# Forming the weight sums in feed-forward block 0 instead of block 1, so that nine blocks of layer 0 use seven products instead of eight

## Chip, cores and metric

The kernel runs on one core of one Trainium2 chip. The metric is the device time of one execution in microseconds (us). Three runs of the kernel before took 1858.07, 1859.28 and 1859.49 us; the median is 1859.28. The execution that was profiled is the one of 1859.49.

## What is computed

Two layers of a graph transformer on N = 2708 tokens with 512 features, 8 heads of 64 and a hidden width of 2048, in float32. Each token attends only to the tokens that the adjacency matrix joins it with (a handful each). Cut to one layer:

```python
q = (h @ Wq.T + bq); k = (h @ Wk.T + bk); v = (h @ Wv.T + bv)      # 8 heads of 64
scores = q k^T / sqrt(64), and -1e9 where adj + eye is 0
ctx = softmax(scores) v
h1 = layer_norm(h + ctx @ Wo.T + bo)
h2 = layer_norm(h1 + relu(h1 @ W1.T + b1) @ W2.T + b2)
```

Layer 1 does the same to the result of layer 0, with its own weights.

## The kernel before

**Tiles and stages.** The tokens are sorted by their number of neighbours and cut into 22 tiles of 128 (the last has 20). In the first stage (up to about 250 us) the kernel finds each token's neighbours and projects keys, values and queries of layer 0. Then comes layer 0's feed-forward, in eleven blocks of two tiles each, numbered k = 0 to 10; the last has the tile of 20 tokens. The loop over blocks is at the end of `by_edges`; inside it, `f` runs over the 16 slices of 128 hidden features. Layer 1 follows in the same manner.

**Attention is interleaved by hand.** The order of instructions on every engine is the order in which the Python code issues them; nothing reorders it. `attend` is a generator. One step of it takes up to two gathered neighbours of each token of a tile (`SLOTS = 2`): VectorE multiplies keys by the query (L1150) and sums within heads (L1156), and weights the values of the step before (L1182, L1189); ScalarE takes the exponentials (L1169) and weights half of the values (L1176). A step is about 4.3 us of VectorE's queue, or 2.7 if it has one neighbour. After a tile's last step come its sums (L1197 to L1212) and, one step later, the division on ScalarE (L1220), which makes the tile's context `cx`. `advance(...)` issues steps after slice f by a credit: the table `PACES` gives it in block 0, `PACE` in other blocks of plain products, and `PACE7` in blocks of seven products; at most three contexts may be ahead. `until(g)` issues whatever steps are missing for tile g.

**A block, on TensorE.** For each slice f, four matmuls make `pf` (L1516 in a plain block, L1648 in a block of seven products) and ScalarE evicts it with a ReLU into `ft` (L1527, L1659). PSUM has three places for `pf` in plain blocks and two in the others. Beside this, each block carries work for its neighbours: at f = 5 to 8 the block before it is finished (its result z is turned, `tp` L1285; then keys and values of layer 1, `k` and `v` at L620, added to their bias by VectorE at L1728 and copied by ScalarE at L1733); from f = 10 the contexts of the next block's two tiles are turned (`tp<-cx`, copied by ScalarE to `cT`, L1290), multiplied by Wo (`o`, L620), added to the residual (`h`, L1447) and normalised (L1269 to L1279); and at f = 15 `h` is turned for the next block. z and h are both called `h` in the profile.

**The second product.** The product with W2 sums over the 16 slices. In a plain block (`feed_forward`), each slice and tile is one matmul of 512 columns (L1489). A block of seven products (`feed_forward_by_seven`) takes slices in pairs j = 0 to 6, and does the 2 x 2 block product of a pair (two tiles by two halves of the columns) with seven matmuls of 256 columns (L1638) instead of the eight that four of 512 columns amount to. The last pair is done plainly (L1670, L1674). For this it needs

- sums of the weights, made once: `form(j)`, four VectorE instructions on 128 x 256 (L1587 to L1590), one of which overwrites a part of W2's tile, and three stores on the SP queue to `form_d` (L1592); each block of seven products loads them back (`ask_forms`, L1605), three of 128 KB for each pair, through three places in SBUF;
- sums of the hidden values, in every such block: `sums(j)`, four VectorE additions of 128 x 128 for each pair (L1620 to L1623), issued at the next even f;
- a tail of eight VectorE instructions (L1693 to L1700), where a plain block has two (L1562).

**Where it is set.** `FORMED` is the block in which the weight sums are formed, after slices f in `FORMS` = (3, 5, 7, 9, 11, 13, 15); blocks FORMED + 1 to 9 then use seven products. It stands in the loop over blocks in four ways:

```python
seven = n == 0 and FORMED < k < NB - 1
if n == 0 and k == FORMED:
    now.prepared()
if n == 0 and k in (FORMED + 1, NB - 1):
    places_of_psum(3 - seven, seven)
...
if n == 0 and k == FORMED and f in FORMS:
    now.form(FORMS.index(f))
```

The first three lines of the loop's choice follow from `seven`: which product is used, which pace (`PACE7 if seven else ...`), and how many PSUM places there are.

Of the kernel before, what the change touches and what calls it, by code (L numbers as in the profile page):

```python
# [52 lines left out]
    (0.75,) * 11 + (0.0,) * 2 + (0.9,) * 3,  # L53
)
PACE7 = (0.0,) * 4 + (0.6, 1.0, 1.5, 1.5, 0.8, 0.7, 0.8, 0.0, 0.0, 0.6, 0.8, 1.4)
FORMED = 1
FORMS = (3, 5, 7, 9, 11, 13, 15)
PACE = (
    (0.0,) * 2 + (0.6,) * 3 + (1.2,) * 4 + (0.6,) * 2 + (0.0,) * 2 + (0.8,) * 3,
# [424 lines left out]
def by_edges(ctx: ExitStack, tc: tile.TileContext, x, xT, adj, layers, out, redo):  # L484
# [34 lines left out]
    def places_of_psum(n, more=False):  # L519

        nonlocal ps_f, ps, ps_s
        stage.close()
        ps_f = stage.enter_context(tc.tile_pool(name="ps_f", bufs=n, space=PSUM))
        ps = stage.enter_context(tc.tile_pool(name="ps", bufs=n, space=PSUM))
        if more:
            ps_s = stage.enter_context(tc.tile_pool(name="ps_s", bufs=1, space=PSUM))
# [767 lines left out]
    class Layer:  # L1294
# [313 lines left out]
        def feed_forward_by_seven(self, k, block, hs, hT):  # L1608
# [5 lines left out]
            fts = []  # L1614
            base = 3 * J * (k - FORMED - 1)

# [259 lines left out]
    for n in range(NL):  # L1876
# [47 lines left out]
        for k, block in enumerate(blocks):  # L1924
# [3 lines left out]
            if n > 0 and 0 < k < NB - AHEAD:  # L1928
                asking = now.queries(blocks[k + AHEAD])
# [5 lines that stand above are left out]
# [4 lines left out]
            for f, zs in enumerate(working):  # L1939
# [25 lines left out]
                if n > 0 and (k, f) == (0, 2):  # L1965
                    now.load_second(1, temp)
                if n == 0 and k == FORMED and f in FORMS:
                    now.form(FORMS.index(f))
# [109 lines left out]
```

## Time and profile before

| | before |
|---|---|
| median of 3 runs | 1859.28 us |
| profiled execution | 1859.49 us |
| its span | 1857.8 us |
| TensorE (PE) busy, share of the span | 1817.6 us, 98% |
| VectorE (DVE) busy | 1460.0 us, 79% |
| ScalarE (ACT) busy | 951.7 us, 51% |
| GpSimd (POOL) busy | 800.3 us, 43% |
| mean granted TensorE clock | 0.991 |
| layer 0's blocks 0 to 9, first matmul of block 0 to first of block 10 | 249.97 to 1034.82 us |

The span is the profiled execution's time on the engines; 1.7 us of the measured time lie around it. The profile cuts the span into 40 slices of 46.4 us and gives each engine's busy share of a slice in tenths (9 is 90% or more). A line of a timeline gives start, duration, engine, line of the code, operation, output and inputs, shapes, the number of records merged in it, and in brackets the idle time before it with what ended that. Each float32 matmul of the program shows as two records. `PEld` are weight loads, `SP` the queue from which most plain transfers are issued.

### The profile page before, as it was taken

Reading aid. Unit: us, or ns where it says so; the run is one execution under the profiler, and the core shown is the slowest. Engines: PE = TensorE matmul, PEld = TensorE weight load, DVE = VectorE, ACT = ScalarE, POOL = GpSimd, SP = SyncE. Lnnn points to the kernel's source line nnn. Section 1 sums busy time; section 2 is a strip of 40 time slices with the busy share of each in tenths; the row PEclk is TensorE's granted clock in tenths of the full one; section 3 lists DMA queues with packets and bytes.
Section 4 is the critical chain, followed back from the end, with each engine's and each line's share of the span. In section 5 each row is a group of like instructions: output and inputs, shape, how many; then the busy total and the mean of one; then the engine's idle time right before and its main releaser. Section 6 shows DMA issues by size and latency. Waiting matters only on the chain.

```text
span 1857.8 us, 22528 instructions
## 1 busy us (share of the span) xinstructions
PE 1817.6 (98%) x6563; PEld 1167.4 (63%) x6563; DVE 1460.0 (79%) x2447; ACT 951.7 (51%) x3271; POOL 800.3 (43%) x745
## 2 busy tenths in 40 slices
PE   9999999999999999989997999999999999999998
PEld 4444466567776777758675644666666666666666
DVE  4986878888978888888878237877988898989853
ACT  4770445545545465454454214555655675566531
POOL 3334755535445454454432013535454554455302
PEclk9999999999999999999998999999999999999999
DMA  9987986756666565665654578735645573655400
GB/s 338 377 329 262 369 273 236 255 173 228 203 201 233 188 215 182 216 211 186 207 157 133 191 245 315 288 132 189 224 162 195 198 261 133 223 194 175 138 23 21
DMA packets 158062, 393.82 MB, mean 212 GB/s; under 512 B 17514, under 2 KB 60894, under 8 KB 157928
## 3 DMA queue, kind: packets, MB, share of 16 engines
q0 software_dynamic: 70608, 252.12, 39.4%
q1 hardware_dynamic: 77162, 118.55, 18.5%
q10 hardware_dynamic: 10158, 21.61, 3.1%
q8 instruction: 54, 0.88, 0.2%
q14 instruction: 80, 0.66, 0.1%
HBM read 338.78 MB, written 53.44 MB: 211 GB/s over the span
## 4 chain that ended last, share of the span: by engine, by line
PE 82%; DVE 9%; ACT 4%; issue 2%; DMA 1%; POOL 1%; POOLq 0%; DVEq 0%; ACTq 0%
PE pf L1516 17%; PE a L1489 16%; PE pf L1648 8%; PE q L620 8%; PE o L620 7%; PE k L620 7%; PE v L620 7%; PE c L1638 4%; PE a L1638 3%; PE tp L1285 2%; DVE sc L1156 2%; DVE kv L1150 2%; ACT kv L1176 1%; DVE acc L1189 1%; ACT cx L1220 1%
## 5 line engine op out<-in xcount | busy, mean ns | idle before, releaser
L1113 POOL DMA_INDIRECT kv<-kv_d,listed x420 | 523.4, 1246 | 331.9 <-DVE acc L1189 161.1
L1516 PE MATMUL pf<-hT,w 128*128 128x256 f32 (+1 forms) x1792 | 393.3, 367 | 0.1
L1516 PEld LDWEIGHTS pf<-hT,w 128*128 128x128 f32 x1792 | 323.5, 190 | 103.2 <-issue 64.4
L1489 PE MATMUL a<-w,ft 128*128 128x512 f32 x800 | 373.2, 592 | 0.0
L1176 ACT ACTIVATE kv<-kv,p 128x64 f32<-128x64 f32 x1232 | 311.0, 335 | 5.0
L1275 POOL TENSOR_TENSOR rd<-va,mhalf 128x1 f32<-128x1 f32 (+1 forms) x88 | 79.6, 905 | 521.2 <-DVE va L1273 521.1
L1150 DVE TENSOR_TENSOR kv<-kv,q 128x1024 f32<-128x1024 f32 (+1 forms) x222 | 256.8, 1157 | 15.0 <-DMA q<-q_d,ident_i 11.1
L1156 DVE TENSOR_REDUCE sc<-kv 128x16 f32<-128x1024 f32 (+1 forms) x222 | 257.9, 1162 | 7.6
L1189 DVE TENSOR_TENSOR acc<-acc,kv 128x1024 f32<-128x1024 f32 (+2 forms) x178 | 205.3, 1153 | 43.6 <-ACT kv L1176 28.3
L1648 PE MATMUL pf<-hT,w 128*128 128x256 f32 x1024 | 232.9, 379 | 0.0
L1489 PEld LDWEIGHTS a<-w,ft 128*128 128x128 f32 x800 | 150.2, 190 | 113.2 <-issue 101.3
L1648 PEld LDWEIGHTS pf<-hT,w 128*128 128x128 f32 x1024 | 194.0, 190 | 33.3 <-issue 8.1
L1527 ACT ACTIVATE ft<-pf,b 128x256 f32<-128x256 f32 (+1 forms) x208 | 94.7, 458 | 196.1 <-PE pf L1516 196.0
L1169 ACT ACTIVATE p<-sc,listed 128x8 f32<-128x8 f32 x420 | 104.4, 297 | 162.1 <-DVE sc L1156 132.9
L620 PE MATMUL o<-wo,cT 128*128 128x512 f32 x336 | 152.8, 599 | 6.5 <-ACT cT L1290 6.5
L1182 DVE TENSOR_TENSOR kv<-kv,p 128x512 f32<-128x512 f32 (+1 forms) x178 | 123.4, 693 | 17.7 <-ACT p L1169 17.7
L1659 ACT ACTIVATE ft<-pf,b 128x256 f32<-128x256 f32 x96 | 44.8, 467 | 152.2 <-PE pf L1648 152.2
L620 PEld LDWEIGHTS o<-wo,cT 128*128 128x128 f32 x336 | 64.0, 192 | 81.9 <-issue 65.7
L1279 DVE SCALAR_TENSOR_TENSOR h<-h,rd,ln_b 128x512 f32<-128x512 f32 (+1 forms) x88 | 66.1, 751 | 46.2 <-POOL rd L1275 46.2
L745 DVE MAX8 tops<-code 128x8 f32<-128x247 f32 (+2 forms) x242 | 79.0, 400 | 28.0 <-ACT code L740 26.0
L1220 ACT ACTIVATE cx<-acc,su 128x64 f32<-128x64 f32 (+1 forms) x352 | 88.2, 333 | 13.9 <-DVE su L1212 10.7
L1447 DVE TENSOR_TENSOR h<-o,xb 128x512 f32<-128x512 f32 (+1 forms) x44 | 30.2, 687 | 76.1 <-PE o L620 67.2
(231 smaller groups left out, 2340.7 us busy)
## 6 DMA issues: line engine op xcount, KB each, us to landing
aj<-in_adj SPq DMA_DIRECT2D x42, 677.0 KB, 6.4
forms<-form_d SPq DMA_DIRECT2D x168, 128.0 KB, 4.0
kv_d<-kvs ACTq DMA_DIRECT2D x21, 512.0 KB, 6.6
xg<-in_xT SPq DMA_DIRECT2D x19, 512.0 KB, 7.3
w<-in_W SPq DMA_DIRECT2D x16, 512.0 KB, 6.2
kv<-kv_d,listed POOLq DMA_INDIRECT x420, 6.1
zT_d<-zT SPq DMA_DIRECT2D x22, 256.0 KB, 6.1
xb_d<-h SPq DMA_DIRECT2D x21, 256.0 KB, 6.0
```

The source lines that it names most:

```text
L620: nc.tensor.matmul(o[:r], xs(c), wm[:, c, :], start=(c == 0), stop=(c == NC - 1))
L1113: return nc.gpsimd.indirect_dma_start(out=to, out_offset=None, in_=table[:, :], in_offset=bass.IndirectOffsetOnAxis(ap=s, axis=0), bounds_ ...
L1150: nc.vector.tensor_tensor(kv[:r, :c, :DM], kv[:r, :c, :DM], self.q[:r].unsqueeze(1).to_broadcast([r, c, DM]), ALU.mult,)
L1156: nc.vector.tensor_reduce(self.sc[:r, s0 : s0 + c, :], kv[:r, :c, :DM].rearrange("p s (h d) -> p s h d", d=DK), AX.X, ALU.add,)
L1176: nc.scalar.activation(to[:, i, hd], kv[:r, i, DM + h * DK : DM + (h + 1) * DK], AF.Copy, scale=p[:r, s0 + i, h : h + 1],)
L1182: nc.vector.tensor_tensor(to[:, 0, :].rearrange("p (h d) -> p h d", d=DK), kv[:r, 0, DM:].rearrange("p (h d) -> p h d", d=DK), p[:r, s0, : ...
L1189: nc.vector.tensor_tensor(self.acc[:r, :c, :], self.acc[:r, :c, :], kv[:r, :c, DM:], ALU.add)
L1220: nc.scalar.activation(cx[:r, hd], self.acc[:r, 0, hd], AF.Copy, scale=self.su[:r, h : h + 1])
L1489: nc.tensor.matmul(a[:r, cols], fts[f][:, c0 : c0 + r], self.w2[f // 2][:, f % 2, cols], start=(f == 0), stop=(f == NFC - 1),)
L1516: nc.tensor.matmul(pf[:, :w], self.w1[f // 2][:, c, f % 2 * P : f % 2 * P + P], hT[:, c, :w], start=(c == 0), stop=(c == NC - 1),)
L1638: nc.tensor.matmul(to, left, right, start=start, stop=stop)
L1648: nc.tensor.matmul(pf[:, :W], self.w1[j][:, c, f % 2 * P : f % 2 * P + P], hT[:, c, :], start=(c == 0), stop=(c == NC - 1),)
```

## The change

One constant is changed:

```diff
-FORMED = 1
+FORMED = 0
 FORMS = (3, 5, 7, 9, 11, 13, 15)
```

The seven sets of weight sums are then formed during block 0, beside its plain products, after the same slices f as before; block 1 becomes a block of seven products, with its sums of hidden values, its loads of the weight sums (21 more transfers of 128 KB), its tail, the pace `PACE7` in place of `PACE`, and two PSUM places for `pf` in place of three. The number of blocks of seven products goes from eight to nine. The order in which the instructions of the changed kernel stand on each engine shows that the steps of attention keep their total of 101 in blocks 0 to 9, and that from block 1 on many of them stand at other places among the blocks' own instructions.

## The prediction

> **What bounds the kernel now.** I read the page's first two parts, then TensorE's waits, then the order of the feed-forward blocks of layer 0 in the timelines of TensorE, VectorE and ScalarE. The page gives the engines' busy time and shares:
>
> ```profile
> PE 1817.6 (98%) x6563; PEld 1167.4 (63%) x6563; DVE 1460.0 (79%) x2447; ACT 951.7 (51%) x3271; POOL 800.3 (43%) x745
> DVE  4986878888978888888878237877988898989853
> PE 82%; DVE 9%; ACT 4%; issue 2%; DMA 1%; POOL 1%; POOLq 0%; DVEq 0%; ACTq 0%
> ```
>
> TensorE is the bound, but VectorE stands at eight tenths beside it through slices 5 to 21, which hold the blocks (232 to 1035 us). The waits of TensorE name where VectorE, or ScalarE behind it, came late (total, times, longest):
>
> ```profile
> PE tp L1285 <- ACT cx L1220: 14.4, 2, 10.0
> PE tp L1285 <- DVE h L1279: 7.8, 5, 2.2
> PE o L620 <- ACT cT L1290: 6.5, 3, 3.4
> ```
>
> Most of these 28.7 us lie in layer 0. The first matmuls of blocks 0 to 10 start at 249.97, 314.12, 392.91, 469.44, 545.02, 627.93, 703.70, 779.46, 866.88, 944.67 and 1034.82, so blocks 0 to 9 last 64.15, 78.79, 76.53, 75.58, 82.91, 75.77, 75.76, 87.42, 77.79 and 90.15 us, 784.85 together. Block 3 has no wait: 75.58 is a block of seven products at TensorE's own pace, and what others have above it is waiting. So layer 0 is a race of two engines, and a change there is worth what both allow.
>
> **The products saved.** Block 1 goes from 64 half products (32 of 512 columns) to 57 (49, and 8 halves of the plain ones). Start, duration, line, shapes and records in block 2:
>
> ```profile
> 462.98 1.88 PE L1670 MATMUL a<-w,ft 128*128 128x512 f32 x4
> 464.69 1.89 PE L1674 MATMUL a<-w,ft 128*128 128x256 f32 x8
> 466.42 0.59 PE L1638 MATMUL a<-forms,ft 128*128 128x256 f32 x2
> ```
>
> Each product is two records; eight of 256 columns take 1.73 us, four of 512 take 1.71, so a half product is 0.43 and seven are 3.02 us. That is all the gain. The weight loads rise by 25 products of two loads at 0.19 us, 9.5 us, and the rows show none of it, since half-width products cost half. [...]
>
> **The weight sums move to block 0.** Four VectorE instructions for each of seven pairs; one set, and where VectorE waits in block 0:
>
> ```profile
> 339.74 0.42 DVE L1587 TENSOR_TENSOR forms<-w 128x256 f32<-128x256 f32 x1
> 340.25 0.42 DVE L1588 TENSOR_TENSOR w<-w 128x256 f32<-128x256 f32 x1
> 340.71 0.43 DVE L1589 TENSOR_TENSOR forms<-w 128x256 f32<-128x256 f32 x1
> 341.18 0.43 DVE L1590 TENSOR_TENSOR forms<-w,forms 128x256 f32<-128x256 f32 x1
> 263.86 1.22 DVE L1150 TENSOR_TENSOR kv<-kv,q 128x1024 f32<-128x1024 f32 x1 [11.05 <-DMA q<-q_d,ident_i]
> 297.53 0.69 DVE L1447 TENSOR_TENSOR h<-o,xb 128x512 f32<-128x512 f32 x1 [1.66 <-PE o L620]
> 304.85 0.69 DVE L1447 TENSOR_TENSOR h<-o,xb 128x512 f32<-128x512 f32 x1 [2.91 <-PE o L620]
> ```
>
> A set is 1.78 us from start to next start. The first hides in the 11.05 us wait for a query. The other six add 10.7 us to a queue that is full from 263.86 to 295.9; the two waits for o, 4.57 us, take them up in part. In the changed order of VectorE two sets stand ahead of the fourth tile's last step, and behind that step on ScalarE stand its division and an eviction that TensorE needs:
>
> ```profile
> 287.94 2.00 ACT L1220 ACTIVATE cx<-acc,su 128x64 f32<-128x64 f32 x8
> 289.85 0.45 ACT L1527 ACTIVATE ft<-pf,b 128x256 f32<-128x256 f32 x1
> 290.35 1.99 PE L1516 MATMUL pf<-hT,w 128*128 128x256 f32 x8
> ```
>
> The pf product already starts the moment ft is out (290.30). Two sets later it waits 2 x 1.78 = 3.5 us. Bounds: 0, if gaps of VectorE swallow the sets, and 5.3 with the clock (below); I take 4.4. Block 0: 68.6 us. VectorE starts the last sums z at 317.84 now; with 10.7 - 4.57 + 0.5 (set 5 or 6 waiting for its predecessor's stores, which land in 4.0) it starts near 324.5. z's two norms take 7.2 us (397.41 to 404.60 in block 2), so the turn of z, which block 1 reaches 10.8 us after its start near 318.6, is ready at 331.8: some 2 us of wait more, where block 1 now has none. The 21 stores of sums move past nothing on SP that block 0 waits for; the loads for block 1 (three, then 18; 2.75 MB more) stand behind the last set's stores, land near 331, and are hidden by z. If VectorE is not late they are what comes last, at most 2 us. POOL's gathers are set by VectorE freeing buffers, and only get later with it.
>
> **VectorE's work.** Block 1 loses 12.4 us of sets and gains 28 additions of 0.26 us to the next start (7.4) and a longer tail (4.1 for 1.4): VectorE's whole work rises by 10.1.
>
> **Where attention's steps fall.** From block 1 on the pace is another, and the steps of VectorE stand elsewhere among TensorE's work: 10, 10, 11, 11, 10, 10, 10, 10, 12 and 7 in blocks 0 to 9, where there were 10, 11, 10, 11, 10, 10, 10, 11, 11 and 7. Blocks 1, 2 and 3 now all have, up to their o product, the sequence that only block 4 has before: the half-width step after the second k, then seven steps and a division on ScalarE ahead of the copy cT. That block shows:
>
> ```profile
> 595.51 5.40 PE L620 MATMUL o<-wo,cT 128*128 128x512 f32 x8 [3.41 <-ACT cT L1290]
> 836.62 1.91 PE L1285 MATMUL tp<-ident,cx 128*128 128x128 f32 x4 [4.37 <-ACT cx L1220]
> ```
>
> The wait is 3.41 us, and the eight records after it take 5.40 instead of 3.60; the granted clock over that block is 0.98, and 0.94 over block 7 with its 4.37 us. So a wait of this kind costs 5.2. [...] Bounds for each of the three blocks: 0 (block 3 before, slack nil) to 5.2; I take 5.2, for the sequence is the same.
>
> By block: 1 is 75.6 + 0.4 (three small transposes) + 2.1 + 5.2 = 83.3. 2: its attention ends in time for z, 80.8. 3: 75.6 + 5.2 + 1.7 = 82.5. 4: it inherits 11 steps, 75.6 + 2.9 = 78.5, and its copy has one step less ahead of it. 5 and 6: 151.7, as before. 7: one step fewer, and the second division earlier, so the waits of 2.20 and 4.37 and the slow clock behind them go: 76.5. 8: 12 steps, with a late second division as block 7 has before, 82.0 (77.8 to 87.4). 9: waits 10.00 at 1005.08 because VectorE must end the last tile; it waits 2.96 for k there, now filled by a step: 87.2. Sum: 68.6 + 83.3 + 80.8 + 82.5 + 78.5 + 151.7 + 76.5 + 82.0 + 87.2 = 791.1, that is 6.2 more than 784.85. Block 10 and layer 1 shift as they are. The profiled execution took 1859.49 us around its span of 1857.8, 0.2 above the median of 1859.28; I add to the first: **1865.7**.
>
> **Rivals.** (a) *VectorE only pays its work.* 10.1 more, less 1.78 in the query wait, 4.57 in block 0 and the 2.85 and 1.18 us that it waits for o in block 1: -0.3, so 1859.2. For it: the total of steps is unchanged. Against: waits move, they seldom vanish. (b) *TensorE sets the end.* If the copies cT come in time in blocks 1 to 3, as in blocks 2 and 3 before, three times 5.2 goes from the sum: -9.4, 1850.1. It decides at 34 us after z's turn: the copy must be done there. Against: block 4's rows. (c) *Waits pile up.* Block 7 keeps its 10.9 us: +17.1, 1876.6. For it: VectorE starts block 1 later than any block before. That the change does not do what it says is out: nine blocks of seven products stand in the order of instructions.
>
> **Numbers.** Forecast, slower by 3.7 to 13 us: 0.52. (a), within 3.7: 0.25. (b), faster by more: 0.12. (c), beyond 13: 0.11. A measurement of this kernel can tell about 0.2%, 3.7 us, from no change: faster 0.12, same 0.25, slower 0.63. The range takes in (a), the forecast and part of both ends: 1853 to 1875, leaving out some 0.17.
>
> **What would show it.** Right: pf of block 0 waits some 3.5 us near 290; z of block 0 starts on VectorE near 324; o waits for cT in blocks 1 to 3; block 7 loses its wait for cx. Wrong: blocks 1 to 3 near 76 us each (then b), or block 10 starting within 3 us of 1034.82 (then a).

## The result, and the profile after

The changed kernel takes 1874.50 us (median of 4 runs, 1873.97 to 1876.22); the kernel before took 1858.67 beside it (4 runs, 1856.20 to 1859.49). The ratio is 1.0089, 95% interval 1.0072 to 1.0106: slower by 15.8 us, or 13 to 20. The forecast was slower by 6.4, at 1865.7. The sign holds and the time lies inside the stated range, just under its upper end, but the size is more than twice the forecast: it falls where the prediction had put (c), beyond 13 us, with a chance of 0.11. The profiled execution is the one of 1873.97, with a span of 1872.2.

The page after, first the busy times, then VectorE's slices:

```profile
PE 1822.7 (97%) x6609; PEld 1177.6 (63%) x6609; DVE 1469.8 (79%) x2481; ACT 953.7 (51%) x3272; POOL 799.7 (43%) x745
...
DVE  5896778878878888898987336877989898998853
```

VectorE has 9.8 us more to do (10.1 were forecast). TensorE is busy for 5.1 us longer, though it has 3.0 us of products less: busy time is also time at a lower clock (in the rows below, eight records at 293.55 take 3.57 us that at full clock take 1.99). Its waits after, in total, times and longest:

```profile
PE tp L1285 <- DVE h L1279: 12.1, 6, 3.4
PE o L620 <- ACT cT L1290: 11.3, 4, 3.4
PE tp L1285 <- ACT cx L1220: 10.3, 2, 9.3
PE pf L1516 <- ACT ft L1527: 3.4, 1, 3.4
```

The wait for `cx` has fallen from 14.4 to 10.3, the others have risen, and the wait of `pf` is new. Now the places. The first matmuls of blocks 0 to 10 start at 249.47, 325.20, 406.47, 488.44, 571.36, 649.20, 727.93, 807.91, 884.16, 963.63 and 1049.05, so blocks 0 to 9 take 799.58 us, 14.73 more than before:

| block | 0 | 1 | 2 | 3 | 4 | 5 | 6 | 7 | 8 | 9 |
|---|---|---|---|---|---|---|---|---|---|---|
| before | 64.15 | 78.79 | 76.53 | 75.58 | 82.91 | 75.77 | 75.76 | 87.42 | 77.79 | 90.15 |
| after | 75.73 | 81.27 | 81.97 | 82.92 | 77.84 | 78.73 | 79.98 | 76.25 | 79.47 | 85.42 |
| change | +11.6 | +2.5 | +5.4 | +7.3 | -5.1 | +3.0 | +4.2 | -11.2 | +1.7 | -4.7 |

Blocks 2 to 9 cancel out (+0.7). Blocks 0 and 1 hold the loss, +14.06. The next two fences give these two stretches of the kernel before and then after: the stretch, its length, the busy time (and instructions) of PE, PEld, DVE, ACT and POOL, the granted clock, the DMA engines' share, and GB/s.

```profile
249.97:392.91 142.94, 142.87 (x492) 89.40 (x492) 116.13 (x165) 77.28 (x290) 72.52 (x62) 1.00 0.72 242
392.91:1034.82 641.91, 614.69 (x2482) 457.57 (x2481) 526.08 (x875) 328.93 (x1214) 274.76 (x225) 0.98 0.59 193
```

```profile
249.47:406.47 157.00, 146.74 (x537) 101.02 (x538) 123.85 (x195) 76.81 (x284) 70.23 (x61) 0.96 0.71 235
406.47:1049.05 642.58, 615.79 (x2481) 455.83 (x2480) 528.48 (x879) 330.62 (x1220) 276.17 (x226) 0.98 0.59 194
```

Length less busy time is TensorE's idle time. In blocks 0 and 1 it was 0.07 and is 10.26. Busy time should have fallen by the 3.02 us of saved products, to 139.85, and is 146.74, with a clock of 0.96 in place of 1.00. So +14.06 is -3.02 for the products, +10.19 of waiting, and +6.89 that the work left takes longer. Most of the 6.89 is slow clock: the granted clock was 0.50 for 3.41 us from 293.37, for 6.83 from 317.26 and for 3.41 from 375.29. The waiting is three rows of TensorE after; the row at 319.48 shows more of the slow clock:

```profile
293.55 3.57 PE L1516 MATMUL pf<-hT,w 128*128 128x256 f32 x8 [3.36 <-ACT ft L1527]
...
318.57 1.11 PE L1285 MATMUL tp<-ident,h 128*128 128x128 f32 x4 [3.38 <-DVE h L1279]
319.48 5.89 PE L1489 MATMUL a<-w,ft 128*128 128x512 f32 x8
...
374.05 5.40 PE L620 MATMUL o<-wo,cT 128*128 128x512 f32 x8 [3.38 <-ACT cT L1290]
```

At full clock these groups take 1.99, 0.60, 3.60 and 3.60, so the four rows hold 6.2 of the 6.89; the remaining 0.7 is not traced. The first and the third of the waits were forecast. The second, the turn of `h` at the end of block 0, was not, and VectorE's rows say where it begins:

```profile
305.55 0.42 DVE L1587 TENSOR_TENSOR forms<-w 128x256 f32<-128x256 f32 x1 [4.79 <-DMA form_d<-forms]
...
312.39 0.42 DVE L1587 TENSOR_TENSOR forms<-w 128x256 f32<-128x256 f32 x1 [0.53 <-DMA form_d<-forms]
```

Set 4 stands in VectorE's queue ahead of the norm of `h`, and may not overwrite its place before set 3's stores have landed. They take some 9 us from the end of the set (296.4), not the 4.0 of the forecast.

### The profile page after: what moved, and what is told of

It is laid out like the page before. It is cut to its first block, busy times and chain, and to the rows that moved or that the text cites. A ratio compares the mean times of both kernels' runs of the same rounds, so it can differ in the third digit from the quotient of the medians.

```text
span 1872.2 us, 22705 instructions
## 1 busy us (share of the span) xinstructions
PE 1822.7 (97%) x6609; PEld 1177.6 (63%) x6609; DVE 1469.8 (79%) x2481; ACT 953.7 (51%) x3272; POOL 799.7 (43%) x745
## 4 chain that ended last, share of the span: by engine, by line
PE 82%; DVE 9%; ACT 4%; issue 2%; DMA 1%; POOL 1%; DVEq 0%; POOLq 0%; SPq 0%; ACTq 0%
PE pf L1516 15%; PE a L1489 15%; PE pf L1648 9%; PE k L620 8%; PE q L620 8%; PE v L620 8%; PE o L620 7%; PE c L1638 5%; PE a L1638 4%; PE tp L1285 2%; DVE sc L1156 2%; ACT kv L1176 2%; DVE kv L1150 2%; ACT cx L1220 1%; DVE acc L1189 1%
## 5 line engine op out<-in xcount | busy, mean ns | idle before, releaser
L1516 PE MATMUL pf<-hT,w 128*128 128x256 f32 (+1 forms) x1664 | 365.0, 367 | 3.6 <-ACT ft L1527 3.4
L1489 PE MATMUL a<-w,ft 128*128 128x512 f32 x736 | 345.7, 596 | 0.0
L1648 PE MATMUL pf<-hT,w 128*128 128x256 f32 x1152 | 262.1, 379 | 0.0
L1489 PEld LDWEIGHTS a<-w,ft 128*128 128x128 f32 x736 | 139.1, 191 | 105.4 <-issue 94.1
L1527 ACT ACTIVATE ft<-pf,b 128x256 f32<-128x256 f32 (+1 forms) x192 | 87.6, 459 | 182.3 <-PE pf L1516 179.5
L620 PE MATMUL o<-wo,cT 128*128 128x512 f32 x336 | 157.5, 614 | 11.3 <-ACT cT L1290 11.3
L1659 ACT ACTIVATE ft<-pf,b 128x256 f32<-128x256 f32 x108 | 50.6, 468 | 179.3 <-PE pf L1648 179.3
L1279 DVE SCALAR_TENSOR_TENSOR h<-h,rd,ln_b 128x512 f32<-128x512 f32 (+1 forms) x88 | 66.1, 751 | 42.0 <-POOL rd L1275 42.0
```

What stands on the lines that cost most here:

```text
L620: nc.tensor.matmul(o[:r], xs(c), wm[:, c, :], start=(c == 0), stop=(c == NC - 1))
L1489: nc.tensor.matmul(a[:r, cols], fts[f][:, c0 : c0 + r], self.w2[f // 2][:, f % 2, cols], start=(f == 0), stop=(f == NFC - 1),)
L1516: nc.tensor.matmul(pf[:, :w], self.w1[f // 2][:, c, f % 2 * P : f % 2 * P + P], hT[:, c, :w], start=(c == 0), stop=(c == NC - 1),)
L1648: nc.tensor.matmul(pf[:, :W], self.w1[j][:, c, f % 2 * P : f % 2 * P + P], hT[:, c, :], start=(c == 0), stop=(c == NC - 1),)
```

## The experiments

The first theory, A: VectorE has no room for the sets in block 0, the stores' landing makes it worse, and all that stands behind them (ScalarE's evictions, the turn of `h`, z) reaches TensorE late. Its rivals: B, attention's steps at other places are the loss, or the transfers are; others are named where they were set out. All times below are medians; each ratio is to the kernel before, run beside it. "0 and 1" is the length of these two blocks, "2 to 9" that of the rest, from the profiled executions.

| kernel | us | ratio, 95% interval | 0 and 1 | 2 to 9 |
|---|---|---|---|---|
| before | 1858.67 | | 142.9 | 641.9 |
| after | 1874.50 | 1.0089 (1.0072 to 1.0106) | 157.0 | 642.6 |
| e1 another place for set 3 and 5 | 1870.11 | 1.0058 (1.0041 to 1.0075) | 153.5 | 642.4 |
| e2 sums early, eight blocks | 1869.11 | 1.0057 (1.0040 to 1.0074) | 154.0 | 641.0 |
| e3 before with the new pace | 1865.69 | 1.0036 (1.0024 to 1.0047) | 149.1 | 642.7 |
| e4 after with the old pace | 1874.69 | 1.0078 (1.0061 to 1.0095) | 160.6 | 641.6 |
| e5 sums on GpSimd | 1872.28 | 1.0080 (1.0066 to 1.0093) | 154.8 | 641.5 |
| e6 Wk, Wv later | 1869.95 | 1.0061 (1.0047 to 1.0074) | 153.3 | 641.8 |
| e7 sets behind the division | 1874.92 | 1.0094 (1.0079 to 1.0109) | 154.4 | 640.8 |
| e8 GpSimd and old pace | 1872.99 | 1.0078 (1.0064 to 1.0091) | 158.4 | 641.3 |
| e9 two steps past h | 1875.32 | 1.0085 (1.0069 to 1.0100) | 153.9 | 648.4 |
| e10 two steps past z | 1873.74 | 1.0080 (1.0066 to 1.0094) | 150.8 | 649.3 |
| e11 stores without sums | 1863.13 | 1.0018 (1.0010 to 1.0027) | 144.8 | 640.8 |
| e12 that, with the old pace | 1863.44 | 1.0021 (1.0012 to 1.0030) | 149.0 | 639.9 |

**e1, e6: the stores.** e1 gives sets 3 and 5 other places, so that no set waits for the stores of the one just ahead; e6 leaves the places and moves two transfers of 1 MB on ScalarE's queue, Wk and Wv. In the changed kernel Wk is issued at 294.52, just ahead of set 3's stores (296.01 to 297.51), and Wv at 305.79, when they have landed.

```diff
-t2, t3, t4 = self.slots if j < NFC // 2 - 2 else self.other_slots
+t2, t3, t4 = self.slots if j not in (3, 5, 6) else self.other_slots
```

```diff
-if (k, f) == (0, 12):      # loads Wk of the next layer
+if (k, f) == (0, 15):
-if (k, f) == (0, 13):      # loads Wv
+if (k, f) == (0, 15):
```

> The changed kernel with sets 3, 5 and 6 of the weight sums in the second group of places, so that set 4 no longer waits for the stores of set 3 (4.79 us) nor set 5 for those of set 4 (0.53). Theory A (the loss is made in block 0: its two TensorE waits of 3.36 and 3.38 us, each with a slow clock behind it, and the second of them only because set 4 waited for stores): h of block 0's successor is ready about 5 us earlier, the second wait goes, block 0 lasts 69 to 71 us instead of 75.7; z of block 0 is then waited for by about 2 us in block 1; 1869 to 1871 us, 4 to 6 below the changed kernel's 1874.5. Rival B (attention's steps stand badly in blocks 1 to 3, and that is the loss): blocks 1 to 3 keep their waits for cT, and the time falls by less than 2 us or not at all.

> The changed kernel with the loads of Wk and Wv of the next layer issued at step 15 of block 0 in place of steps 12 and 13. Theory A: set 3's stores land 9 us late because they share the transfer engines with these two megabytes. Then set 4's wait of 4.79 us falls below 1 us, h is turned in time, and the time is that of e1: 1868 to 1872 us. Theory B: the stores are late by themselves or by the gathers of keys, which stay: the wait stays above 3.5 us, and the time is 1873 to 1877.

Measured: 1870.11 and 1869.95, both some 4.5 below the changed kernel, as A had it. The turn of `h` waits in neither. What e6 changed shows in the stretch where set 4 waits; first after, then e6:

```profile
300.00:305.00 5.00, 5.00 (x20) 3.21 (x19) 0.76 (x1) 1.14 (x4) 0.00 (x0) 1.00 0.85 307
```

```profile
300.00:305.00 5.00, 5.00 (x20) 3.12 (x19) 3.72 (x8) 1.32 (x5) 0.00 (x0) 1.00 0.37 122
```

The last three columns are the clock, the share of the DMA engines and GB/s. With Wk and Wv elsewhere the share falls from 0.85 to 0.37, the stores land in time (0.8 us of wait is left), and VectorE works for 3.72 of these 5 us in place of 0.76. So the wait for the stores is real, it is the other transfers that stretch it (by the times of issue it is Wk), and it costs 4.5 us. In e1, TensorE's wait shifts to the turn of z:

```profile
331.75 0.66 PE L1285 MATMUL tp<-ident,h 128*128 128x128 f32 x4 [1.83 <-DVE bo L1333]
```

With that one term right, e1 is what the prediction described: block 0 takes 69.1 us (forecast 68.6), z starts on VectorE at 324.35 (forecast 324.5) and its turn waits 1.83 (forecast 2.1). But the time is still 11 above before.

**e2, e3, e4: the sums early, and the places of steps, apart.** e2 forms the sums in block 0 and leaves block 1 plain, with the old pace. (Its block 1 then multiplies by a part of W2 that the sums have overwritten, so the result is not that of the two layers; the instructions of block 1 are those of a plain block.) e3 is the kernel before with `PACE7` in block 1, which puts all later steps where the changed kernel has them. e4 is the changed kernel with block 1 on the old pace, which puts the steps from block 2 on where they were.

```diff
-seven = n == 0 and FORMED < k < NB - 1
+seven = n == 0 and SEVEN <= k < NB - 1          # e2: SEVEN = 2
```

```diff
-advance((PACE7 if seven else (PACE if k else PACES)[n])[f])
+advance((PACE7 if seven or (n, k) == (0, 1) else (PACE if k else PACES)[n])[f])      # e3
+advance((PACE7 if seven and k > 1 else (PACE if k else PACES)[n])[f])                # e4
```

> The weight sums are formed in block 0, but block 1 stays a plain block, as before; seven products from block 2 on. No product is saved, and from block 2 on the steps of attention stand as in the kernel before. Theory A (loss made in block 0): block 0 lasts about 75.7 us (11.6 more than before), block 1 about 78.8, and the later blocks win back little: 1867 to 1871. Rival B (the loss comes from where the steps stand): 1859 to 1862, since they stand as before. Rival C (VectorE's total work sets the end): no work is added, so 1859 to 1861.

> The kernel before, with the pace of seven products in its block 1: only the places of attention's steps change, and from block 2 on they are those of the changed kernel. Theory A: the waits for cT come in blocks 2 and 3 (81 to 83 us each) and are given back in blocks 4, 7 and 9, so the time is 1857 to 1862. Rival B (placing is the loss): blocks 2 and 3 gain 12 us and little is given back: 1866 to 1872.

> The changed kernel with the plain pace in block 1: from block 2 on the steps of attention stand as in the kernel before; block 0 and the products are those of the changed kernel. Theory A: block 0 lasts 75.7 us as in the changed kernel, blocks 2 to 9 together as before, block 1 76 to 81 us: 1867 to 1874. Rival B: the waits for cT of blocks 1 to 3 go, 1858 to 1862.

Measured: 1869.11, 1865.69 and 1874.69. e2 lies in A's range: the move of the sums alone costs 10.3, and its blocks 0 and 1 take 11.1 more, with VectorE's whole work the same as before (1460.3 us busy for 1460.0). So C is out: it is where the work stands, not how much there is. e3 lies between the ranges of A and B, and its 6.9 us for places alone look like a point for B. But its blocks say otherwise: 2 to 9 take 642.7, only 0.8 more than before, and the loss is in block 1, which takes 85.05 in place of 78.79. Nearly all of that is one wait for `cT`, which A had left out, with the slow records behind it (3.60 at full clock):

```profile
368.11 6.56 PE L620 MATMUL o<-wo,cT 128*128 128x512 f32 x8 [3.14 <-ACT cT L1290]
```

Block 1 is a plain block in e3, so the pace alone makes this wait. e4, 0.7 above A's range, says the same from the other side: blocks 2 to 9 go back to the old places and to 641.6, and nothing is won; block 1 has lost its wait for `cT` and got one of 3.50 for `zT` (348.16), whose eight records take 6.66. B is out for blocks 2 to 9: there these two sequences of steps trade one wait for another and cost the same. In block 1 the places do cost.

**e5, e7, e8: the sets off VectorE, or behind the division.** e5 is e1 with the four subtractions of `form` on GpSimd. e7 is e1 with sets 1 and 2 moved behind the fourth tile's division. e8 is e5 with e4's pace.

```diff
-nc.vector.tensor_tensor(t3, b22, b12, ALU.subtract)       # e5, and so the other three
+nc.gpsimd.tensor_tensor(t3, b22, b12, ALU.subtract)
```

```diff
-FORMS = (3, 5, 7, 9, 11, 13, 15)                          # e7, with two places in turn
+FORMS = (3, 9, 10, 11, 12, 13, 15)
```

> The changed kernel with the weight sums formed by GpSimd in place of VectorE, in the places of e1 (sets in turn in two groups of places). Theory A: TensorE's waits in block 0 are the sets' time on VectorE, handed on by ScalarE's queue. Then the 3.37 us wait of pf near 293 and the slow clock after it go, the turn of h is in time, block 0 comes back to 64 to 66 us and only block 1's wait for cT is left: 1861 to 1865 us. Theory B: the loss is made by the stores and loads of sums among the other transfers, whoever forms the sums: 1868 to 1872, like e1. Theory D: GpSimd is slow at it and its gathers queue behind the sets, so that VectorE waits for keys instead: 1870 to 1880.

> e1 with sets 1 and 2 not formed ahead of the fourth tile's division but behind it: sets 0 to 6 at steps 3, 9, 10, 11, 12, 13 and 15, in two groups of places in turn. Theory A: VectorE is full from 264 us to the turn of h, so a set moved there moves the wait: pf's 3.37 us near 293 go, and the turn of h waits 3 to 5 us instead: 1868 to 1873 us. Theory C: only the sets ahead of the division cost, VectorE has room behind it: 1863 to 1866.

> e5 with block 1 on the pace that it has in the kernel before, so that the steps of attention stand from block 2 on as they stand there. Theory A: with the sets off VectorE, z of block 0 is in time and neither block 0 nor block 1 waits; the saved products then show: 1855 to 1859 us. Theory A with a wait for z or cT in block 1 left: 1860 to 1865. Theory B: the pace does nothing, as in e4, and the transfers cost what they cost: 1867 to 1873.

Measured: 1872.28, 1874.92 and 1872.99. e5 failed A's forecast and lies in D's range, but by another way than D said; B's range ends only 0.3 below it. VectorE did not wait for keys; it waited for the norm's one-column power `rd`, which is GpSimd's and stood behind the sets there:

```profile
312.11 1.21 DVE L1279 SCALAR_TENSOR_TENSOR h<-h,rd,ln_b 128x512 f32<-128x512 f32 x1 [8.37 <-POOL rd L1275]
```

The old queue's wait came back in the new queue, and the turn of `h` waits 3.80 there. e7 goes as A said, with 2 us more than its range: the wait of `pf` is gone, and the turn of `h` has it,

```profile
317.19 1.12 PE L1285 MATMUL tp<-ident,h 128*128 128x128 f32 x4 [5.37 <-DVE h L1279]
```

after 2.21 at 311.16 for its first tile. (Its profiled execution is the lowest of four, 1869.47; the median is 5.4 above it, so the table's time and the rows are to be read apart.) A part of that wait is once more a store: sets at consecutive f come too soon for two places, and set 3 waits 4.57 for its place. e8 was A's hope of 1855 to 1859, and failed: blocks 0 and 1 take 158.4, with the waits of e5 and e4's wait for `zT` (3.88). Its time lies in B's range, but these waits are not for transfers.

**e9, e10: two steps of attention later.** e9 is e7 and e6 together with no steps at f = 10 and 11 of block 0; e10 is e1 with none at f = 14 and 15.

```diff
-(0.0,) * 4 + (0.85,) * 8 + (0.0,) * 2 + (0.8,) * 2,
+(0.0,) * 4 + (0.85,) * 6 + (0.0,) * 4 + (0.8,) * 2,       # e9
+(0.0,) * 4 + (0.85,) * 8 + (0.0,) * 4,                    # e10
```

> e7 with the loads of Wk and Wv at step 15 as in e6, and with no attention at steps 10 and 11 of block 0, so that two double steps of VectorE (8.8 us) go from ahead of the turn of h to block 1, and 18 steps stand ahead of block 1 in place of 20. Theory A: block 0 waits because VectorE has more to do ahead of the turn of h than the time allows, 10.7 us of sets; with 8.8 us of steps gone from there, none of pf, the turn of h and the turn of z waits over 1 us, block 0 falls to 64 to 67 us, and what is left is what block 1 and later blocks pay for the two steps: 1856 to 1863 us if their VectorE has room, 1864 to 1870 if a copy cT waits there once more. Theory E: the waits are made by the sets' stores and W2's readers and not by VectorE's work: block 0 stays over 70 us, 1869 to 1876.

> e1 with no attention at steps 14 and 15 of block 0: the two double steps that stand between the turn of h and the sums z go to block 1. Theory A: z of block 0 starts some 8 us earlier than in e1 (near 316 us), the wait of 1.83 us for the turn of z goes, pf's wait of 3.37 us stays, and block 1, with 12 steps, keeps its wait for cT: 1866 to 1870 us. Theory F: the late z is what costs, and with it in time the wait for cT goes too: 1860 to 1864.

Measured: 1875.32 and 1873.74, both above every range of A; e9's time lies in E's range, and F (1860 to 1864) is out. In e9 block 0 does get shorter as A said, from 73.3 in e7 to 68.7 (64 to 67 were expected; the turn of `h` still waits 2.09, again behind a store). In e10 it takes 69.4, as in e1 (69.1), and the turn of z no longer waits. But the two steps are paid for later. In e9 block 1 waits for the division of a tile that now comes late,

```profile
373.43 1.91 PE L1285 MATMUL tp<-ident,cx 128*128 128x128 f32 x4 [6.82 <-ACT cx L1220]
```

(e10 waits 2.45 there), and blocks 2 to 9 take 648.4 and 649.3, 6 to 9 us more than in the other kernels, though 81 steps fall to them as in the changed kernel (VectorE's busy time there is 532 us for 528.5): here the steps stand at yet other places, and this time no wait elsewhere goes in return. E's time is right and its way is not, since block 0 fell below 70; and A was too hopeful of what block 1 and the later blocks can take in.

**e11, e12: the stores without the sums.** The last pair takes VectorE's 12.4 us of sets out of block 0: the places are filled once with a constant, and the 21 stores of them stay. Since no set holds them back, the stores leave earlier, from 255 to 280 us, where the changed kernel sends them from 259 to 329.

```diff
+nc.gpsimd.memset(place[:, : 6 * W], 0.5)
...
-nc.vector.tensor_tensor(t3, b22, b12, ALU.subtract)
-nc.vector.tensor_tensor(b12, b12, b11, ALU.subtract)
-nc.vector.tensor_tensor(t2, b22, b12, ALU.subtract)
-nc.vector.tensor_tensor(t4, b21, t2, ALU.subtract)
```

> The changed kernel without the 28 subtractions that form the weight sums: their places are filled once by GpSimd with a constant and stored as before, so the 21 stores, the loads and the nine blocks of seven products stay, and VectorE has 12.4 us less to do in block 0. It leaves the weight sums out, so the seven products multiply by a constant in their place. Theory A: VectorE's work in block 0 is what the change pays for there. Then pf, the turn of h and the turn of z wait for nothing, block 0 takes 64 to 65 us, and block 1 keeps its wait for cT: 1859 to 1863 us. Theory B: the stores and what they share the queues with make the loss: 1867 to 1873.

> e11 with block 1 on the pace that it has in the kernel before, which puts attention's steps from block 2 on where they stand there; the weight sums are left out as in e11. Theory A: with 12.4 us of VectorE's work gone from block 0 no wait is left in blocks 0 and 1, and the 3.0 us of saved products show: 1854 to 1857.5 us, the best that nine blocks of seven could give. Theory A with block 1 too full of VectorE's work for 11 steps beside its sums of pairs: a wait for z's turn, cx or cT in block 1, 1859 to 1864.

Measured: 1863.13 and 1863.44. e11 is 11.4 below the changed kernel, 0.1 above the top of A's range, and B (1867 or more) is out. Block 0 takes 64.94, where it took 64.15 before. Its blocks 0 and 1:

```profile
249.80:394.58 144.78, 140.72 (x537) 97.90 (x538) 112.57 (x167) 76.29 (x284) 71.12 (x62) 1.00 0.74 254
```

Idle time is 4.06 in place of 10.26, of which 3.38 is the forecast wait in block 1, and busy time is 140.72, within 0.9 of the 139.85 that the products leave. (Its profiled execution, of 1860.49, is 2.6 below the median, and the clock stayed at 1.00 behind that wait; the median may hold more slow clock.) So the traffic of 21 stores and the loads costs next to nothing when no set waits for it; what block 0 pays for is VectorE's time. That time has two parts: e1 and e6 price the waits of sets for stores at 4.5, and the 7.0 from e1 to e11 are left for the sets' own 12.4 us, though e11 also moves the stores, which no run here separates. e12 missed A's best case, 1854 to 1857.5, and lies in its other one: z is turned without a wait, at 326.68, but its copy `zT` comes late for the keys:

```profile
336.81 5.40 PE L620 MATMUL k<-wk,zT 128*128 128x512 f32 x8 [4.28 <-ACT zT L1290]
```

The copy stands on ScalarE behind a step of attention and a division (330.94 to 335.39), and that step had waited 5.48 for VectorE's scores. In block 1 before the same step and division stand there too, but z is turned 16.0 us after the block's start, not 11.0, and the keys come later.

Even with weight sums for nothing, nine blocks of seven products do not beat eight: e11 and e12 are some 4 us slower than before, which took 1859.19 beside them.

## Why the prediction was right in sign and wrong in size

**Right, by their rows.** The products saved: the busy time of e11's blocks 0 and 1, at full clock, is within 0.9 of what -3.02 leaves. VectorE's work: +9.8 for +10.1. The first set hides in the wait for a query, which falls from 11.05 to 3.65. The wait of `pf` near 290: 3.36 at 293.55 and 1.6 of slow clock, 4.9 for 4.4. The waits for `cT` in blocks 1, 2 and 3: 3.38, 3.42 and 3.42, with prices of 5.2, 6.4 and 5.2 for 5.2 each. Block 7 lost its waits: 76.25 for 76.5. Blocks 2, 3 and 4 came within 1.2.

**The step that failed.** It is the 0.5 us of "set 5 or 6 waiting for its predecessor's stores, which land in 4.0". The wait fell on set 4 and took 4.79, with 0.53 more for the set after it. The 4.0 stands in the page before for the loads of the sums (`forms<-form_d`); of the stores of block 1 before, the profile tells the landing of two, 1.8 and 4.5 us after their issue. In block 0 set 3's stores share the engines with Wk and the gathers and take some 9. How full the engines are does not tell it alone: their share is 0.83 over those 9 us, and 0.93 from 353 to 368 in block 1 before. Behind set 4 on VectorE stands the norm of `h`, which the prediction had not priced at all, since it took block 0's end to be z; the turn of `h` waits 3.38, and the slow clock makes it 6.2, where the sum had nothing. Block 0 took 75.7 for 68.6. e1 and e6 take this wait away by two different means, and both give back 4.5.

**Block 1 and z.** z started at 328.89 for 324.5, but its turn didn't wait, since TensorE was late itself; block 1 took 81.27 for 83.3. In e1, where block 0 is on the forecast, z and its wait are as forecast, and block 1 takes 84.4.

**Blocks 5 and 6** were put at "151.7, as before" and took 158.7. The prediction counted 10 steps in each, as before, and so costed them at nothing. But the steps stand at other places: VectorE comes to the last sums of the block ahead 3 to 4 us later (in block 5 they start 3.4 us after its first matmul, where they started 0.7 ahead of it), and in each the turn of z waits; here block 5's:

```profile
662.62 0.66 PE L1285 MATMUL tp<-ident,h 128*128 128x128 f32 x4 [2.21 <-DVE h L1279]
```

That explains 4.4 of the 7.0. Another 1.2 is in block 6, where the four records that turn `cx` at 779.57 take 1.76 in place of 0.60, while ScalarE's division (778.94 to 780.94) is still making it. The rest lies in rows that name no wait, at a clock of 1.00, and stays open. Against it blocks 8 and 9 took 4.3 less than forecast. With the two misses, +7.1 in block 0 and +7.0 in blocks 5 and 6, less 5.7 in the others, the sum of 791.1 becomes the measured 799.58.

**The rivals.** (a), that VectorE only pays its work, 1859.2, fell: its slack lies in other places than the new work. (b), that TensorE sets the end and copies come in time, fell by the three rows for `cT`. (c) named nearly the right time, 1876.6, and the wrong cause: block 7 did not keep its 10.9 us. What piled up was in block 0.

**What the forecast's sum hid.** It has 5.2 for the places of steps in each of blocks 1 to 3, and takes most of it back in blocks 4, 7 and 9; its blocks 2 to 9 come to 639.2, for 641.9 before. The loss there is real, and so is what pays for it: over blocks 2 to 9 the old sequence and the new one both take 640 to 643 us, in twelve kernels. (That places can matter there, e9 and e10 show, with two other sequences and some 7 us.) The price of the change is in blocks 0 and 1, and its parts add up: 10.3 for the sums early (e2) and 6.9 for the pace (e3), less 3.0 of products, are 14.2 of the 15.8. They are made by 12.4 us of sets where VectorE is full from 264 us to z but for its waits for stores, which e11 gives back together with these waits, and a block 1 that waits for `cT` with the new pace, as it does in e3 without any sums of pairs, or for `zT` with the old one. No kernel here with nine blocks of seven products got rid of a wait in block 1.

## What to carry to other kernels

Where two engines are both nearly full, ask of moved work not what it adds to the busy time but what stands behind it in the queue of the place that it moves to. Here 12.4 us of sets, with VectorE's busy time the same, made block 0 10.6 us longer in e2 (74.76 for 64.15), of which 4.92 is one wait and 2.2 the slow records behind it, while the slack left in block 1 was worth nothing (79.28 for 78.79). A store's landing time read in one stage did not hold in a stage where other transfers ran: 1.8 and 4.5 us in block 1 before, some 9 in block 0 of the changed kernel; another place for the buffer that is written again soon (e1) and those transfers elsewhere (e6) each gave back 4.5. And before a wait is moved to another queue, look what small thing of the critical chain lives there: in e5 the norm waited 8.37 us for `rd`.

## What the runs showed of the hardware

- **The same wait has different prices.** After 3.38 to 3.42 us of idle time, the eight records of TensorE that follow took 3.70 (e5 at 373.69), 5.40 (after, 374.05), or 6.53 (after, 454.89), against 3.60 at full clock. After a wait of 2.21 us the four records of a turn took 1.12 in the kernel before (958.10), where the granted clock was 0.50 from 958.05, and 0.66 in the changed kernel (662.62), where it stayed at 1.00. From 250 to 1050 us the granted clock of these two kernels drops to 0.50 for 3.41, 6.83 or 10.24 us at a time, and in the changed kernel the first three of these stretches begin at 293.37, 317.26 and 375.29, beside waits that end at 293.55, 318.57 and 374.05. What decides the price of a wait, no run here shows.
- **The sets were slower on GpSimd, and VectorE was slower beside it.** In e5 the same subtraction of 128 x 256 takes 0.71 to 1.71 us on GpSimd, where VectorE takes 0.42, and beside it VectorE's own L1279 takes 1.21 (at 312.11) in place of 0.75. In the changed kernel one L1622 (337.73) takes 0.70 in place of 0.28 beside another instruction of GpSimd on whole rows (L607, 1.54 us from 337.63). What makes them longer, no run here separates.
- **An overwrite waited for a reader.** In the changed kernel, set 0's second subtraction (L1588) overwrites weights of W2 and waited 5.75 us (to 258.40) for TensorE's product L1489 to have read them. It cost nothing only because a wait for a query stood in the same place (11.05 us in the kernel before).
